# Two on-chip buffers merged, a third ring lengthened, and one small exponential moved in a two-layer graph-attention kernel

## The chip, the cores and the metric

The kernel runs on one core of a Trainium2 chip. Such a core has a matrix engine (PE), which multiplies and whose weight loads are recorded as a row of their own (PEld), a vector engine (DVE), a scalar engine (ACT), a general engine (POOL), and a queue that issues transfers (SP). Each engine works through its own list of instructions in order; engines wait for each other through semaphores. The metric is the device time of one execution in microseconds (us): lower is better. The kernel before takes 2965.63 us (median of three runs, 2965.52 to 2966.96).

## The reference

Sixty-four independent graphs of 256 nodes with 512 features each pass through two layers, and each layer is a residual with a layer norm around it:

```
x = layernorm(x + relu(attention_0(x, adj)))
x = layernorm(x + attention_1(x, nodemask, adj))

attention_0: feats = x W  (8 heads of 64);  s_i = feats.a_self,  n_j = feats.a_neigh
             att = softmax_j(leaky_relu(s_i + n_j, 0.2) where adj, else -1e10);  out = att feats + b
attention_1: q, k, v = x W_qkv  (8 heads of 64)
             att = 0.33 softmax(q k^T / 8) + 0.33 adj + 0.33 exp(-adj);  out = (att v) W_out + b_out
```

All of it is float32.

## The kernel before

One graph is one batch `b`; a batch is 128 partitions by two row tiles. The loop over `b` is a software pipeline: in round `b`, the two functions `attention0_beside_projections1(b)` and `attention1_beside_projections0(b)` run parts of up to five batches beside each other, among them layer 0's attention of batch `b`, layer 1's softmax of batch `b-1`, layer 1's output of batch `b-2` and layer 0's features of batch `b+1`. They are lists of `do(stage, batch, step)` calls, and after every call `in_order()` ties each new instruction behind the one before it on its engine. So the order in which a step stands in the list is the order on PE, ACT, DVE and SP alike. All loads and stores of the loop are issued by SP.

The projections use a scheme with seven products in place of eight (`seven`, lines 292 to 325). Of its products, p1, p6, p7 and p4 are summed up in one PSUM bank, the "chain": after p1 the bank is copied out by ACT (line 320), and only then may PE add p6 into the same bank, and so on. The p2 product has a bank of its own, p5 and p3 share a third. For the output projection (`po`, layer 1's last product) the copies go to the tile `o`; the left factors that are sums, `oC`, are made on DVE in two steps, `half_blocks` 0 and 1 (lines 285 to 290). PE's order in that projection is p1, p2, p6, p5, p7, then the row sums `pd` of the softmax, then p4 and p3.

In the stretch before it, PE computes the scores of layer 1, `pz`, for four pairs of heads g = 0 to 3 (`scores`, line 857), and between g = 1 and g = 2 the products of the previous batch's probabilities with its values (`values`, `av`, line 973). ACT turns each `pz` into `p` with two exponentials (line 871), one for each half of the keys. DVE adds the two halves to `both` (line 883).

The tiles named `p` come from a ring of four buffers with the tag "p". A batch has four of them, one per pair of heads, so the first exponential of a batch waits until `values` has read the first `p` of the batch before.

Layer 0's attention needs factors along the rows of the next batch: PE transposes them (`pr`, line 82), DVE takes a maximum and a bias `nb` from it (lines 499 and 500), ACT forms an exponential of 8 x 256 numbers into `grow` (`broadcast` part 0, line 506), DVE clamps it (`broadcast` part 1, line 510), SP writes it to DRAM (`gs`, line 514) and reads it back spread over all 128 partitions (`gb`, line 515, 1028 KB). The next readers are `nd` (line 559), from which ACT forms `ccol` (line 566), and the weights `pT` (line 667).

The rows of `x` for the residual are loaded by `load_rows` (line 138, 512 KB) into a buffer with the tag "x", of which there is one; they are read by `end` (line 733) in the next round. The tile `hb`, layer 0's output in blocks, has a buffer of its own with the tag "hb"; it is written by four transfers in `blocks` (line 114, from the DRAM copy `hs`) and read by DVE's transpose `hT` (line 121). In the list, `load_rows(b + 1)` stands directly behind `blocks`.

Of the kernel before, what the change touches and what calls it, by code (L numbers as in the profile page):

```python
# [8 lines left out]
FT = mybir.dt.float32  # L9
# [8 lines left out]
def kernel(  # L18
# [30 lines left out]
    P = 128  # L49
    NB, N, F = x.shape  # L50
    H, _, U = w0.shape
    T = N // P
    C = F // P
    HG = H // 2
    UA = U + 1
    UX = U + 2
# [8 lines left out]
    io = ctx.enter_context(tc.tile_pool(name="io", bufs=3))  # L65
    work = ctx.enter_context(tc.tile_pool(name="work", bufs=2))
# [40 lines left out]
    X, XB, ADJB, MROW = {}, {}, {}, {}  # L107
# [26 lines left out]
        nc.sync.dma_start(MROW[b], nodemask[b].partition_broadcast(P))  # L134

    def load_rows(b):
        X[b] = io.tile([P, T, F], FT, tag="x", name=f"x_{b}", bufs=1)
        nc.sync.dma_start(X[b], x[b].rearrange("(t p) f -> p t f", p=P))


    mask_sb = io.tile([NB, N], U8, tag="mask", name="mask_sb", bufs=4)
    nc.sync.dma_start(mask_sb, nodemask)
    X[0] = io.tile([P, T, F], FT, tag="x", name="x_0", bufs=1)
    for t in range(T):
        nc.sync.dma_start(X[0][:, t, :], x[0, t * P : (t + 1) * P, :])
    C2, F2 = C // 2, F // 2

    wf_sb = consts.tile([P, 7, C2, HG, UX], FT, name="wf_sb")
    wf12 = work.tile([P, C2, HG, UX], FT, tag="p", name="wf12", bufs=4)
    wf = [[wf_sb[:, 0], wf12], [wf_sb[:, 1], wf_sb[:, 2]]]  # L150
    def load_wf(engine, g):
        for c in range(C):
# [57 lines left out]
    nc.vector.tensor_scalar_mul(m33, pm, L_BOTH)  # L210


    maskz = io.tile([NB, N], FT, tag="hb", name="maskz", bufs=1)
    nc.vector.transpose(maskz, maskf)
    def right_factors(w, w12):

# [23 lines left out]

    def load_weights1():

        wk1 = work.tile([P, C2, F], FT, tag="p", name="wk1", bufs=4)
        wv12 = work.tile([P, C2, F2], FT, tag="both", name="wv12", bufs=4)
        parts = w_qkv.rearrange("(k c p) (h s u) -> s k c p h u", k=2, p=P, s=3, u=U)

        def get(dst, s, k, heads=slice(0, H)):
            for c in range(C2):
                nc.sync.dma_start(
                    dst[:, c].rearrange("p (h u) -> p h u", u=U), parts[s, k, c][:, heads]  # L250
                )

        get(wqk_sb[:, 0], 0, 0)
        get(wqk_sb[:, 1], 0, 1)
        get(wk1, 1, 0)
        get(wqk_sb[:, 6], 1, 1)
        get(wv_sb[:, 0], 2, 0, slice(0, HG))
        get(wv12, 2, 0, slice(HG, H))
        get(wv_sb[:, 1], 2, 1, slice(0, HG))
        get(wv_sb[:, 2], 2, 1, slice(HG, H))  # L260

        def combine(part):
            q1, q2, s1, s2, s3, s4, k2 = (wqk_sb[:, i] for i in range(7))
            if part == 0:
                nc.vector.tensor_add(s1, wk1, k2)
                nc.vector.tensor_sub(s2, s1, q1)
            elif part == 1:
                nc.vector.tensor_sub(s3, q1, wk1)
            elif part == 2:
                nc.vector.tensor_sub(s4, q2, s2)  # L270
            else:
                right_factors(wv_sb, wv12)
            in_order()

        return combine
# [379 lines left out]
    def attend0(b):  # L655
        pT = {}

        def weights(h):


            tag = "pT" if h < HG else "both" if b > 1 or h > HG + 1 else "p"
            if (b, h) == (0, H - 1):
                pT[h] = work.tile([P, T, N], FT, tag="rec1", name=f"pT_{b}_{h}", bufs=1)
            else:
                pT[h] = work.tile([P, T, N], FT, tag=tag, name=f"pT_{b}_{h}", bufs=4)
            for j in range(T):
                nc.vector.scalar_tensor_tensor(  # L667
                    pT[h][:, j, :],
                    GB[b][h],
                    CCOL[b][:, j, h : h + 1],  # L670
                    AT[b][:, j, :],
                    op0=ALU.max,
                    op1=ALU.mult,
                )

        AV = {}

        def product(g, t):


            if t == 0:
                AV[g] = psum.tile([P, T, F], FT, tag="sc", name=f"av0_{b}_{g}", bufs=2)
            av = AV[g][:, t, : HG * UA].rearrange("p (h u) -> p h u", u=UA)
            half = P // 2
            for k in range(HG):
                h = g * HG + k
                for j in range(T):
                    for r in range(2):
                        i = t * P + r * half
                        matmul(  # L690
                            av[r * half : (r + 1) * half, k, :],
                            pT[h][:, j, i : i + half],
                            V0[b][:, j, h, :UA],
                            start=(j == 0),
                            stop=(j == T - 1),
                        )

        REC0 = {}

        def rec0(g):  # L700
            REC0[g] = small.tile([P, T, HG], FT, tag="rec", name=f"rec0_{b}_{g}")
            av = AV[g][:, :, : HG * UA].rearrange("p t (h u) -> p t h u", u=UA)
            nc.vector.reciprocal(REC0[g], av[:, :, :, U])  # L703

        def norm0(g, t):
            if b not in X1:
                X1[b] = io.tile([P, T, F], FT, tag="x1", name=f"x1_{b}", bufs=1)
            av = AV[g][:, t, : HG * UA].rearrange("p (h u) -> p h u", u=UA)
            if b < 1:
                rec = small.tile([P, HG], FT, tag="rec", name=f"rec0_{b}_{g}_{t}")  # L710
                nc.vector.reciprocal(rec, av[:, :, U])
                s = slice(g * HG * U, (g + 1) * HG * U)
                nc.vector.tensor_mul(
                    X1[b][:, t, s].rearrange("p (h u) -> p h u", u=U),
                    av[:, :, :U],
                    rec.unsqueeze(2).to_broadcast([P, HG, U]),
                )
                return
            for k in range(HG):
                h = g * HG + k  # L720
                nc.scalar.activation(  # L721
                    X1[b][:, t, h * U : (h + 1) * U],
                    av[:, k, :U],
                    AF.Copy,
                    scale=REC0[g][:, t, k : k + 1],
                )

        def end(ts=slice(0, T)):
            if ts.start == 0:
                NORM["l0", b] = LayerNorm(X1[b], b, "l0")  # L730
            ln = NORM["l0", b]
            for t in range(ts.start, ts.stop):
                nc.vector.scalar_tensor_tensor(
                    X1[b][:, t, :],
                    X1[b][:, t, :],
                    0.0,
                    X[b][:, t, :],
                    op0=ALU.max,
                    op1=ALU.add,
                    accum_out=ln.sums[:, t : t + 1],  # L740
                )
            ln.mean(ts)
            if ts.stop == T:
                X.pop(b)

        return dict(
            weights=weights,
            product=product,
            rec0=rec0,
            norm0=norm0,  # L750
            end=end,
            squares=lambda *ts: NORM["l0", b].squares(*ts),
            norm=lambda *ts: NORM["l0", b].apply(*ts),
        )
# [83 lines left out]

    def softmax1(b):
        PROBS[b] = [  # L840
            work.tile([P, 2, T, N], FT, tag="p", name=f"p_{b}_{g}", bufs=4)
            for g in range(HG)
        ]
        both = {}
# [102 lines left out]
    def attend1(b):  # L947
        if b < NB - 1:
            oT = work.tile([P, C, N], FT, tag="oT", name=f"oT_{b}", bufs=1)
        else:  # L950
            oT = io.tile([P, C, N], FT, tag="x", name=f"oT_{b}", bufs=1)
        av = {}

        def weights(g):
# [180 lines left out]
    def do(stage, b, step, *args):  # L1135

        if 0 <= b < NB:
            if (stage, b) not in S:
                S[stage, b] = stages[stage](b)
            S[stage, b][step](*args)  # L1140
            in_order()
# [93 lines left out]
    def attention0_beside_projections1(b):  # L1235
# [69 lines left out]
        do("proj0", b + 1, "product", "p7")  # L1305
        do("attend0", b, "norm")
        do("proj1", b, "blocks")
        if b + 1 < NB:
            load_rows(b + 1)
        do("proj0", b + 1, "add", 22)  # L1310
        do("proj0", b + 1, "product", "p2")
        if b + 2 < NB:
# [8 lines left out]
    def attention1_beside_projections0(b):  # L1321
# [12 lines left out]
        do("softmax1", b - 1, "scores", 2)  # L1334
        do("softmax1", b - 1, "scores", 3, 0)
        do("proj0", b + 1, "rows")
        do("proj0", b + 1, "broadcast", 0)
        do("softmax1", b - 1, "scores", 3, 1)
        do("attend1", b - 2, "half_blocks", 1)
        do("proj0", b + 1, "broadcast", 1)  # L1340
        do("softmax1", b - 1, "both", 2)
        do("softmax1", b - 1, "both", 3)
        do("attend1", b - 2, "product", "p1")
        do("attend1", b - 2, "product", "p2")
        do("proj1", b, "hT")
        do("attend1", b - 2, "product_add", 11)
# [7 lines left out]
        do("attend1", b - 2, "product", "p4")  # L1354
        do("proj0", b + 1, "bias")
        do("softmax1", b - 1, "inverted")
        do("attend1", b - 2, "product", "p3")
        do("attend1", b - 2, "product_add", 12)
        if b == 1:
# [129 lines left out]
```

## Time and profile before

| what | value |
|---|---|
| median of three runs | 2965.63 us |
| the profiled execution, its own time | 2965.2 us |
| its span, first to last instruction | 2963.4 us |
| mean granted PE clock | 0.994 of full speed |
| round of the loop (start of `pz` to start of `pz`, 1491.10 to 1536.09) | 44.99 us |
| mean DMA rate | 122 GB/s |
| the first 150 us: PE clock, PE busy | 0.91, 128.22 us |
| the last 94 us: PE clock, PE busy | 0.94, 80.97 us |

The span is the time from the first to the last instruction of the program; the execution's own time lies 1.8 us above it. The profile shows for each engine how long it was busy, for each wait who ended it, and in the timeline when each group of instructions began. Nearly all of the span is made of 62 like rounds; a time that recurs in every round counts some 62-fold. Times in the prediction such as 1546.21 are microseconds from the start of the span, and most belong to the round that begins at 1536.09.

### The profile page before, as it was taken

What the parts mean: (1) busy time and instruction counts of PE and PEld (TensorE: products, weight loads), DVE (VectorE), ACT (ScalarE), POOL (GpSimd) and SP (SyncE); (2) the same over time, 40 slices, a digit from 0 to 9 for tenths busy, and PEclk for the clock granted to TensorE, in tenths of its full rate; (3) what the DMA queues carried; (4) which work ended last, traced back from release to release, by engine and by line L of the source; (5) the groups of instructions that cost most, each with busy time, mean ns of one, the idle gap of its engine ahead of it and who ended that gap; (6) DMA issues with size and microseconds to landing.
All of it is one profiled execution on the core that took longest, in us unless ns stands there. A gap on an engine that the chain in (4) does not pass through costs nothing.

```text
span 2963.4 us, 67973 instructions
## 1 busy us (share of the span) xinstructions
PE 2906.6 (98%) x26302; PEld 2468.6 (83%) x26302; DVE 2600.9 (88%) x5147; ACT 1779.5 (60%) x4905; POOL 209.9 (7%) x526
## 2 busy tenths in 40 slices
PE   8899999999999999999999999999999999999998
PEld 6788888888888888888888888888888888888886
DVE  5798988988989989989989889889899899899884
ACT  2556665666666666566666656666666666666563
POOL 0000000000000000000000000000000000000001
PEclk8999999999999999999999999999999999999999
DMA  6445445454454454454454554554544544545532
GB/s 126 94 123 123 121 135 123 118 139 114 121 138 116 120 142 115 122 130 119 131 123 119 138 123 115 141 113 121 139 115 120 138 117 125 126 121 133 123 101 68
DMA packets 778872, 362.24 MB, mean 122 GB/s; under 512 B 694604, under 2 KB 696636, under 8 KB 762552
## 3 DMA queue, kind: packets, MB, share of 16 engines
q1 hardware_dynamic: 776440, 357.37, 47.6%
q8 instruction: 210, 3.44, 0.5%
q14 instruction: 110, 0.90, 0.1%
q10 hardware_dynamic: 2112, 0.52, 0.1%
HBM read 289.42 MB, written 68.13 MB: 121 GB/s over the span
## 4 chain that ended last, share of the span: by engine, by line
PE 73%; DMA 12%; ACT 7%; SPq 4%; DVE 3%; issue 1%; POOL 0%; DVEq 0%; ACTq 0%; POOLq 0%
PE pq_p L311 27%; PE pv_p L311 13%; PE po_p L311 10%; PE pf_p L311 9%; PE av L690 8%; DMA x<-in_x_dram 6%; DMA hs<-x 4%; SPq L114 4%; ACT p L871 3%; ACT x L382 2%; PE pd L891 2%; PE pz L857 1%; PE av L973 1%; DVE xT L121 1%; ACT v L320 1%
## 5 line engine op out<-in xcount | busy, mean ns | idle before, releaser
L311 PE MATMUL pq_p<-hC,wqk_sb 128*128 128x128 f32 x4096 | 493.3, 279 | 5.3 <-ACT qk L320 3.6
L311 PEld LDWEIGHTS pq_p<-hC,wqk_sb 128*128 128x128 f32 x4096 | 468.7, 192 | 22.3 <-ACT qk L320 17.7
L667 DVE SCALAR_TENSOR_TENSOR pT<-gb,ccol,at 128x256 f32<-128x256 f32 x992 | 403.0, 477 | 55.3 <-ACT ccol L566 55.3
L871 ACT ACTIVATE p<-pz,hide 128x512 f32<-128x512 f32 x512 | 315.4, 685 | 140.8 <-PE av L973 123.8
L311 PE MATMUL pq_p<-hT,wqk_sb 128*128 128x128 f32 x3072 | 366.2, 276 | 1.4 <-DVE hT L121 0.7
L311 PEld LDWEIGHTS pq_p<-hT,wqk_sb 128*128 128x128 f32 x3072 | 360.1, 193 | 5.5 <-DVE hT L121 1.2
L963 DVE TENSOR_TENSOR p<-p,ct 128x1024 f32<-128x1024 f32 x252 | 308.7, 1225 | 8.6
L721 ACT ACTIVATE x<-av,rec 128x64 f32<-128x64 f32 x1008 | 221.0, 336 | 151.4 <-DVE rec L703 151.4
L956 DVE TENSOR_TENSOR p<-p,rb 128x1024 f32<-128x1024 f32 x252 | 304.2, 1207 | 4.9 <-DMA rb<-rs 4.9
L311 PE MATMUL po_p<-wo_sb,oC 128*128 128x256 f32 x992 | 240.9, 386 | 21.2 <-ACT o L320 21.2
L690 PE MATMUL av<-v,pT 128*64 128x65 f32 x8192 | 256.7, 223 | 1.1 <-DVE pT L667 0.6
L857 PE MATMUL pz<-qk 64*128 64x256 f32 x2048 | 256.2, 389 | 0.9 <-ACT p L871 0.9
L690 PEld LDWEIGHTS av<-v,pT 128*64 128x64 f32 x8192 | 246.9, 138 | 10.2 <-issue 2.5
L626 ACT ACTIVATE v<-v 128x64 f32<-128x64 f32 x1024 | 251.7, 338 | 0.0
L311 PE MATMUL pf_p<-wf_sb,xC 128*128 128x264 f32 x992 | 251.3, 386 | 0.0
L311 PE MATMUL pv_p<-wv_sb,hC 128*128 128x256 f32 x1024 | 244.2, 381 | 4.1 <-ACT v L320 4.1
L857 PEld LDWEIGHTS pz<-qk 64*128 64x128 f32 x2048 | 187.1, 186 | 65.5 <-ACT p L871 26.1
L311 PEld LDWEIGHTS po_p<-wo_sb,oC 128*128 128x128 f32 x992 | 183.3, 190 | 68.7 <-ACT o L320 46.1
L973 PE MATMUL av<-p,v 128*64 128x256 f32 x2016 | 231.9, 382 | 0.2 <-DVE p L963 0.2
L320 ACT COPY v<-pv_p 128x256 f32<-128x256 f32 x256 | 95.6, 373 | 226.1 <-PE pv_p L311 225.9
L883 DVE SCALAR_TENSOR_TENSOR both<-p 128x512 f32<-128x512 f32 x256 | 170.3, 683 | 60.7 <-ACT p L871 60.7
L311 PEld LDWEIGHTS pv_p<-wv_sb,hC 128*128 128x128 f32 x1024 | 195.4, 191 | 32.7 <-ACT v L320 4.9
(163 smaller groups left out, 4453.8 us busy)
## 6 DMA issues: line engine op xcount, KB each, us to landing
rb<-rs SPq DMA_DIRECT2D x63, 1024.0 KB
gb<-gs SPq DMA_DIRECT2D x62, 1028.0 KB
hs<-x SPq DMA_DIRECT2D x64, 512.0 KB
xb<-in_x_dram SPq DMA_DIRECT2D x252, 128.0 KB
x<-in_x_dram SPq DMA_DIRECT2D x63, 512.0 KB
hb<-hs SPq DMA_DIRECT2D x252, 128.0 KB
y<-hs SPq DMA_DIRECT2D x63, 512.0 KB
out_dram<-y SPq DMA_DIRECT2D x63, 512.0 KB
```

The source lines that it names most:

```text
L311: matmul(d, lhsT, rhs, start=(p in FIRST and i == 0), stop=(i == len(todo) - 1), skip_group_check=True,)
L320: nc.scalar.copy(out[COPIES[p]], dst)
L626: nc.scalar.activation(V0[b][:, t, h, :U], V0[b][:, t, h, :U], AF.Copy, scale=V0[b][:, t, h, U : U + 1],)
L667: nc.vector.scalar_tensor_tensor(pT[h][:, j, :], GB[b][h], CCOL[b][:, j, h : h + 1], AT[b][:, j, :], op0=ALU.max, op1=ALU.mult,)
L690: matmul(av[r * half : (r + 1) * half, k, :], pT[h][:, j, i : i + half], V0[b][:, j, h, :UA], start=(j == 0), stop=(j == T - 1),)
L721: nc.scalar.activation(X1[b][:, t, h * U : (h + 1) * U], av[:, k, :U], AF.Copy, scale=REC0[g][:, t, k : k + 1],)
L857: matmul(pz[:, r, j, :], QK[b][rows, g, 1, j * P : (j + 1) * P], QK[b][rows, g, 0, :], start=True, stop=True,)
L871: nc.scalar.activation(p[:, :, j, :], pz[:, :, j, :], AF.Exp, bias=hide[:, j, b : b + 1], scale=U**-0.5,)
L883: nc.vector.scalar_tensor_tensor(both[g], p[:, :, 0, :], TINY, p[:, :, 1, :], op0=ALU.add, op1=ALU.add)
L956: nc.vector.tensor_mul(p, p, REC[b][:, k : k + 2, g // 2, :] .unsqueeze(2) .to_broadcast([P, 2, T, N]),)
L963: nc.vector.tensor_add(p, p, CT[b].unsqueeze(1).to_broadcast([P, 2, T, N]))
L973: matmul(av[0][r * U : (r + 1) * U, g % 2, :], V1[b][:, j, 2 * g + r, :], PROBS[b][g][:, r, j, :], start=(j == 0), stop=(j == T - 1),)
```

## The change

The change has four edits that go together.

1. The ring "p" of layer 1's probabilities gets a fifth buffer.
2. To make room, the tag "x" goes: `x`'s rows now take the same single buffer as `hb` (tag "hb"). The two tiles that had used these buffers at the edges of the program move: `maskz` from "hb" to "y", and the last batch's `oT` from "x" to "xC".
3. Since `x`'s rows of batch b+1 can be written only when `hb` of batch b has been read, `load_rows(b + 1)` moves from behind `blocks` to the end of the round, behind `inverted`, that is behind the transfers `rs` and `rb`.
4. `broadcast` part 0 (the exponential into `grow`) moves from in front of the last exponential of `p` to behind the output projection's p1 with its copy; part 1 (the clamp, and the transfers `gs` and `gb`) moves behind `both` of g = 2. In the list p1 itself moves up, in front of `broadcast`; PE's order stays.

```diff
     def load_rows(b):
-        X[b] = io.tile([P, T, F], FT, tag="x", name=f"x_{b}", bufs=1)
+        X[b] = io.tile([P, T, F], FT, tag="hb", name=f"x_{b}", bufs=1)
         nc.sync.dma_start(X[b], x[b].rearrange("(t p) f -> p t f", p=P))
...
-    maskz = io.tile([NB, N], FT, tag="hb", name="maskz", bufs=1)
+    maskz = io.tile([NB, N], FT, tag="y", name="maskz", bufs=1)
...
         PROBS[b] = [
-            work.tile([P, 2, T, N], FT, tag="p", name=f"p_{b}_{g}", bufs=4)
+            work.tile([P, 2, T, N], FT, tag="p", name=f"p_{b}_{g}", bufs=5)
             for g in range(HG)
         ]
...
-            oT = io.tile([P, C, N], FT, tag="x", name=f"oT_{b}", bufs=1)
+            oT = work.tile([P, C, N], FT, tag="xC", name=f"oT_{b}", bufs=1)
...
         do("proj1", b, "blocks")
-        if b + 1 < NB:
-            load_rows(b + 1)
         do("proj0", b + 1, "add", 22)
...
         do("softmax1", b - 1, "scores", 3, 0)
         do("proj0", b + 1, "rows")
-        do("proj0", b + 1, "broadcast", 0)
         do("softmax1", b - 1, "scores", 3, 1)
         do("attend1", b - 2, "half_blocks", 1)
+        do("softmax1", b - 1, "both", 2)
+        do("attend1", b - 2, "product", "p1")
+        do("proj0", b + 1, "broadcast", 0)
         do("proj0", b + 1, "broadcast", 1)
-        do("softmax1", b - 1, "both", 2)
         do("softmax1", b - 1, "both", 3)
-        do("attend1", b - 2, "product", "p1")
         do("attend1", b - 2, "product", "p2")
...
         do("softmax1", b - 1, "inverted")
+        if b + 1 < NB:
+            load_rows(b + 1)
         do("attend1", b - 2, "product", "p3")
```

The lines left out change the first batch's `x_0` to the tag "hb" and `bufs=4` to `bufs=5` at the other tiles of the ring "p". No arithmetic is added or taken away. On ACT the order of a round was: both exponentials of g = 2, the first of g = 3, `grow`, the second of g = 3, copy of product p1. It becomes: both of g = 2, both of g = 3, copy of product p1, `grow`. On DVE it was: `half_blocks` 1, clamp, `both` 2, `both` 3. It becomes: `half_blocks` 1, `both` 2, clamp, `both` 3.

More of the change, by code (lines that the diff above doesn't have):

```diff
@@ L142 @@
     nc.sync.dma_start(mask_sb, nodemask)
-    X[0] = io.tile([P, T, F], FT, tag="x", name="x_0", bufs=1)
+    X[0] = io.tile([P, T, F], FT, tag="hb", name="x_0", bufs=1)
     for t in range(T):
@@ L148 @@
     wf_sb = consts.tile([P, 7, C2, HG, UX], FT, name="wf_sb")
-    wf12 = work.tile([P, C2, HG, UX], FT, tag="p", name="wf12", bufs=4)
+    wf12 = work.tile([P, C2, HG, UX], FT, tag="p", name="wf12", bufs=5)
     wf = [[wf_sb[:, 0], wf12], [wf_sb[:, 1], wf_sb[:, 2]]]
@@ L241, in load_weights1 @@
     def load_weights1():
-        wk1 = work.tile([P, C2, F], FT, tag="p", name="wk1", bufs=4)
+        wk1 = work.tile([P, C2, F], FT, tag="p", name="wk1", bufs=5)
         wv12 = work.tile([P, C2, F2], FT, tag="both", name="wv12", bufs=4)
@@ L664, in weights @@
             else:
-                pT[h] = work.tile([P, T, N], FT, tag=tag, name=f"pT_{b}_{h}", bufs=4)
+                pT[h] = work.tile(
+                    [P, T, N], FT, tag=tag, name=f"pT_{b}_{h}", bufs=5 if tag == "p" else 4
+                )
             for j in range(T):
```

## The prediction

> **What bounds the kernel now.** First the page's part 1 (busy time by engine), then the waits (total us, times, longest).
>
> ```profile
> PE 2906.6 (98%) x26302; PEld 2468.6 (83%) x26302; DVE 2600.9 (88%) x5147; ACT 1779.5 (60%) x4905; POOL 209.9 (7%) x526
> ```
>
> ```profile
> ACT p L871 <- PE av L973: 123.8, 61, 2.0
> ...
> PE po_p L311 <- ACT o L320: 21.2, 62, 0.7
> ...
> PE pv_p L311 <- ACT v L320: 5.0, 4, 2.3
> ...
> DVE nd L559 <- DMA gb<-gs: 3.6, 7, 1.0
> ```
>
> PE sets the time. Only one of its waits recurs in every round: 62 times before `po_p`, for ACT's copy `o`. The idle column gives 0.34 us each, but the ends of matmuls are modelled, so I measure from start to start, in PE's timeline (start, length, group):
>
> ```profile
> 1523.72 1.89 PE L311 MATMUL pv_p<-wv_sb,hT 128*128 128x256 f32 x8
> 1525.45 2.75 PE L311 MATMUL pv_p<-wv_sb,hC 128*128 128x256 f32 x12
> 1528.04 1.05 PE L311 MATMUL pf_p<-wf_sb,xT 128*128 128x264 f32 x4
> ...
> 1543.99 1.89 PE L311 MATMUL po_p<-wo_sb,oT 128*128 128x256 f32 x8
> 1546.21 2.86 PE L311 MATMUL po_p<-wo_sb,oC 128*128 128x256 f32 x12 [0.33 <-ACT o L320]
> 1549.00 1.07 PE L891 MATMUL pd<-both,ones 128*32 128x256 f32 x16
> ```
>
> Two projections of the same form. `pv_p` runs unhindered: eight records in 1525.45 - 1523.72 = 1.73 us, 0.216 each, twelve in 2.59. `po_p` takes 2.22 for its eight (0.49 more) and 2.79 for its twelve (0.20 more). Of that 0.20 I put half to the restart behind the stop and half to the change of shape at `pd`: where `po_p` restarts behind `pd` without waiting for ACT, its four records take 1505.98 - 1505.01 = 0.97 instead of 0.86, so a restart costs 0.10. **The stop thus costs 0.49 + 0.10 = 0.59 us a round, 62 x 0.59 = 36.6 us**, not the 21.2 of the idle column.
>
> Why ACT is late (ACT's timeline of that stretch):
>
> ```profile
> 1542.80 1.84 ACT L871 ACTIVATE p<-pz,hide 128x512 f32<-128x512 f32 x3 [0.27 <-PE pz L857]
> 1544.87 0.47 ACT L506 ACTIVATE grow<-pr,nb 8x256 f32<-8x256 f32 x1 [0.22 <-issue]
> 1545.24 0.66 ACT L871 ACTIVATE p<-pz,hide 128x512 f32<-128x512 f32 x1
> 1545.81 0.34 ACT L320 COPY o<-po_p 128x256 f32<-128x256 f32 x1
> 1547.38 0.37 ACT L320 COPY o<-po_p 128x256 f32<-128x256 f32 x1 [1.22 <-PE po_p L311]
> ```
>
> `grow` waits 0.22 for its bias `nb` (DVE, 1544.64 + 0.14) and then takes a slot; the last exponential and the copy stand behind it.
>
> **The moved exponential.** Back-to-back exponentials start 0.57 apart (four in 2.42, the next ACT group 2.29 behind the first: 1539.15 to 1541.44). The three from 1542.80 last to 1544.64, so the third (0.69 long) starts at about 1543.96. Without `grow` the fourth starts at 1544.53, not 1545.24, and the copy at 1545.10, not 1545.81. The copy's input is there: p1 is the first four of PE's eight records, over at 1543.99 + 3 x 0.216 + 0.38 = 1545.02. It ends at 1545.44, and with today's hand-off (1546.15 to 1546.21) PE may go on at 1545.50. Unhindered, p6's matmul is due at 1543.99 + 8 x 0.216 = 1545.72, and its weight load one slot ahead, at 1545.50. **So the stop goes whole, with no margin left for the weight load**; a slip of 0.1 would cost up to 6 us of the 36.6. What is late next on PE: p7's wait for p6's copy. It passes unhindered today (twelve records without an inner gap beyond those named), and keeps its distance, since p6's end and its copy move together; `grow` (about 1545.4 to 1545.9) is over before the copy of p6 at about 1546.8.
>
> **What stands behind `grow`.** DVE: clamp (0.27), `both` 3, the transpose `hT`. DVE now takes `both` 2 (0.67) at 1545.38 and reaches the clamp at about 1546.0, when `grow` is done; the same three operations fill the same time, and `hT` starts at 1546.79 as before. Cost 0. DVE also has 1.19 us idle at 1549.5 before the next `o` sum (it waits for ACT's copy of p7); 0.59 of it goes, so it does not bound.
>
> SP: `gs` starts at 1546.3 instead of 1545.68, 0.62 later, and `nd` is wanted 0.59 earlier:
>
> ```profile
> 1541.02 0.67 SPq L138 DMA_DIRECT2D x<-in_x_dram  x1
> 1541.79 2.62 SPq L114 DMA_DIRECT2D adj<-in_adj_dram  x4
> 1544.45 0.74 SPq L134 DMA_DIRECT2D mask<-in_nodemask_dram  x1
> 1545.68 0.31 SPq L514 DMA_DIRECT2D gs<-grow  x1
> 1547.59 0.34 SPq L515 DMA_DIRECT2D gb<-gs  x1
> ...
> 1554.55 0.16 DVE L559 TENSOR_TENSOR nd<-v,gb 128x16 f32<-128x16 f32 x1
> ```
>
> From `gs` to `gb` 1.91; from `gb`'s issue to `nd`, in rounds where `nd` did wait for it, 5.5 to 5.9 (1419.99 - 1414.44 in one), 7.3 and 7.5 in two of them. So `nd` can start at 1546.3 + 1.9 + 5.7 = 1553.9, and is wanted at 1553.96. Beyond that it has cover: `ccol` starts only at 1555.44, behind ACT's `qk` copy, 0.73 behind `nd`'s end, so about 0.65 of lateness costs nothing; then `pT`, whose last ends at 1562.7 for the matmul that reads it at about 1563.8, about 1 us more. Cost 0, though `nd`'s 7 waits will be more.
>
> **x's rows.** Their issue (0.67) and 512 KB leave the stretch in front of `gs`: its DMA share is 0.92 (1541.0 to 1547.6). In some rounds SP itself brings `gs` late (1591.61, 1.2 behind its clamp), and there the missing issue gives back what the clamp takes. The new place is behind `rb`, at about 1556 in this round's terms, where DMA stands at 0.54 and then 0.01 (1566.0 to 1575.3). `rb`, wanted at 1565.27, is issued before x (1556.08) and is waited for once in the whole span. The store `out` and the load `y` behind x come 1.5 to 2 us later (that stretch moves 182 GB/s at a share of 0.54, some 340 KB per us at full share, and x has 512 KB); `y` is issued at 1562.39 and wanted at 1572.17: covered.
>
> Here a rule speaks against the change. The Trainium skill, "Trainium Kernel Development and Optimization", section Best Practices, wants buffers doubled so that DMA and compute overlap; the shared buffer does the reverse: x can't land before `hT` has read `hb`, nor `hb` before `end` has read x. By the rule a load of 4.2 us (x's step in the chain of waits, 1541.02 to 1545.24) would be exposed: 62 x 4.2 = 260 us slower. By the row, x's first reader starts at 1570.61, 14 us behind the new issue, and `hb`'s transfers at 1538.22 come 12 us after that reader in their round. I take 0. (That step itself is an inferred link: in the next round x is issued at 1587.23 and the copy still comes 3.6 us later, so nothing on ACT waits for x.)
>
> **The fifth buffer.** It ends ACT's 2.03 us wait in front of the first exponential (61 in 123.8 us). "Perfetto Trace Analysis", section Optimization Strategy, reads a gap that recurs on the engine that should be saturated as a sign of too little SBUF; taken for ACT that would promise 124 us. But ACT is 60% busy, and by the rows nothing on PE comes sooner: scores of g = 2 start at 1541.62, directly behind `values`, and the exponential at 1542.80 waits for those scores. Value 0; DVE gets its first two `both` up to 1 us earlier, and waits for PE's `pr` instead.
>
> **Sum**: 2965.2 (the profiled execution) - 36.6 = 2928.6; the median lies 0.4 above it, and I leave 1 us for slips at the weight load: **2930 us**.
>
> **Rivals.**
>
> *The gain is given back at the next hand-off* (10%). PE already waits a little for ACT's `qk` copy before `pq`'s p6 (1555.59; 17.7 us in all on the weight load). If ACT's chain there (`zd`, copy, two squares, `qk`) kept its times, PE would lose again what it gained: 2965, or 2947 if half. Against it: `zd` waits for DVE's `inv`, which follows the `o` sum, which follows PE's p7; that chain moves with PE.
>
> *A smaller slip at the copy* (within the 80% below): if ACT's copy, now the first to carry the wait for the transpose of `xb`, comes 0.1 to 0.2 late, 62 x 0.1 to 0.2 comes back: 2935 to 2941.
>
> *Slower through `gb`* (4%). Place: `nd`. Its price is 62 us for each us beyond cover. It decides once `gs`-to-`gb`-to-`nd` takes over 1553.96 + 0.65 + 1.0 - 1546.3 = 9.3 us in most rounds (8.6 to 9.8 with the roughness of the cover), and makes the kernel slower than before once it also eats 0.59, at 9.9; at 10.5 the time is 2965 + 37 = 3002. For: two rounds had 7.5 behind `gb` alone. Against: the usual 7.4 to 7.8, and a less loaded stretch.
>
> *The change does nothing* (4%): `grow` only trades places and the copy is held by something the trace puts down to ACT: 2965.
>
> **Numbers.** Whole or nearly whole gain 80%, given back in part 6%, in whole 4%, nothing 4%, slower by `gb` or a transfer 4%, more than the stop (rounds at the DMA-late end gain too, up to 2922) 2%. The range runs from 2924 to 2946. A measurement tells 0.2% (6 us) from no change: faster 0.88, same 0.08, slower 0.04.
>
> **What would show it.** Right: PE's wait for `o` gone from its list; `po_p`'s eight records 1.73 apart from the twelve; round 44.4; ACT's first exponential 2 us earlier without effect; `nd` waiting for `gb` in many rounds, by under 0.7. Wrong: the stop unchanged or moved to `pq_p`; `pT` or `av` (line 690) waiting for `gb`; `end` (line 733) waiting for x.

## The result, and the profile after

The changed kernel takes 2945.48 us (median of four runs, 2943.05 to 2947.07); the kernel before, measured again beside it, 2966.15. The ratio is 0.9929, with a 95% interval of 0.9912 to 0.9947. So it is faster by 20.7 us, inside the stated range but 0.5 us below its upper end, where 36.6 us had been forecast as the gain of the path. The profiled execution of the changed kernel has a span of 2943.7 us (2945.5 us in all), at a granted clock of 0.994 as before.

The page after, parts 1 and 4:

```profile
PE 2893.2 (98%) x26302; PEld 2475.2 (84%) x26302; DVE 2595.7 (88%) x5147; ACT 1784.6 (61%) x4905; POOL 210.1 (7%) x526
...
PE 95%; DVE 2%; issue 1%; DMA 1%; ACT 1%; SPq 0%; POOL 0%; DVEq 0%; POOLq 0%; ACTq 0%
```

The chain that ended last now stays on PE for 95% of the span, where it was 73%: the link over ACT's copy, and with it the links over transfers that had been inferred behind it, are gone. The same place in PE's timeline of the changed kernel, in the same round of the loop:

```profile
1532.16 1.89 PE L311 MATMUL po_p<-wo_sb,oT 128*128 128x256 f32 x8
1533.89 2.75 PE L311 MATMUL po_p<-wo_sb,oC 128*128 128x256 f32 x12
1536.58 1.07 PE L893 MATMUL pd<-both,ones 128*32 128x256 f32 x16
```

The eight records and the twelve are 1.73 us apart, as `pv_p`'s are, and no idle time stands behind the line. ACT in that stretch:

```profile
1530.97 2.42 ACT L873 ACTIVATE p<-pz,hide 128x512 f32<-128x512 f32 x4 [0.48 <-PE pz L859]
1533.27 0.39 ACT L320 COPY o<-po_p 128x256 f32<-128x256 f32 x1
1533.52 0.46 ACT L506 ACTIVATE grow<-pr,nb 8x256 f32<-8x256 f32 x1
```

Four exponentials in one piece, then the copy, then `grow`. The usual round, from `pr` to `pr`, is 44.39 us long; it was 44.98. The difference of 0.59, in 62 rounds, is the 36.6 us of the forecast. But the span shrank by 19.7 only. What took the rest is in the waits (total us, times, longest):

```profile
ACT p L873 <- PE av L975: 37.3, 61, 0.6
...
PE av L692 <- issue: 12.6, 9, 2.1
...
DVE nd L559 <- DMA gb<-gs: 3.9, 9, 0.8
...
PE pq_p L311 <- issue: 2.0, 2, 1.2
```

Two lines are new: PE stops 11 times on "issue", 14.6 us of idle in all, some 16.8 from start to start. "Issue" is time in which an engine waits for no instruction that the profile shows. One of the stops, in PE's timeline:

```profile
1548.73 3.95 PE L692 MATMUL av<-v,pT 128*64 128x65 f32 x128
1552.61 0.38 PE L311 MATMUL pq_p<-hC,wqk_sb 128*128 128x128 f32 x1
1554.20 1.94 PE L311 MATMUL pq_p<-hC,wqk_sb 128*128 128x128 f32 x15 [1.21 <-issue]
```

The sixteen matmuls of one product are broken after the first; those behind it need nothing that the first did not have. It is no wait for data. All of these stops lie 21 to 23 us behind the round's `pr`, and they come 4, 7 or 11 rounds apart. What lies there among the transfers (SP's timeline, then three stretches: window, length, busy time of PE, PEld, DVE, ACT and POOL, PE clock, DMA share, GB/s):

```profile
1543.66 0.31 SPq L939 DMA_DIRECT2D rb<-rs  x1
1544.02 0.43 SPq L138 DMA_DIRECT2D x<-in_x_dram  x1
1545.78 0.39 SPq L1113 DMA_DIRECT2D out_dram<-y  x1
1552.42 0.36 SPq L989 DMA_DIRECT2D y<-hs  x1
```

```profile
1544.40:1548.50 4.10, 4.10 (x39) 4.10 (x38) 4.10 (x11) 4.10 (x13) 0.00 (x0) 1.00 0.93 265
1548.50:1552.20 3.70, 3.70 (x121) 3.58 (x121) 3.39 (x9) 2.03 (x8) 0.00 (x0) 1.00 0.86 277
1552.20:1555.60 3.40, 2.19 (x31) 1.93 (x26) 3.37 (x7) 1.75 (x8) 0.00 (x0) 1.00 0.45 157
```

`rb`, x's rows and the store follow each other without a pause for over 7 us, and PE runs dry at the end of that burst. The page's part 3 lists the queue q8, kind "instruction", with 210 packets and 3.44 MB, 16384 bytes a packet. PE's records show that these are PE's own instructions, 256 to a packet. From one stop to the next PE goes through 3328, 5888 or 9216 records (matmuls, weight loads and its waits for semaphores), which is exactly 13, 23 or 36 times 256, and just as many packets of q8 start in between. So every stop lies at a seam between two packets' worth of instructions; in the other kernels below that stop, all stops lie on the same seams. A round has 836 records, 3.27 packets' worth, so a seam comes back to nearly the same place of the round after 4, 7 or 11 rounds. Counting q8's packets, in 60 rounds, by the time since the round's `pr`:

```
started in            before   changed
12.0 to 19.0 us         30        14
19.0 to 21.0 us         23        58
21.0 to 23.0 us         42         3
```

In the changed kernel the burst ends about 20 us behind `pr`, hardly a packet of instructions starts while it lasts (8 in 61 bursts, their last microsecond left out), and 58 start within the 2 us around its end. Each of the stops ends 2.2 to 2.5 us after such a packet has begun (1551.87 for the one shown).

The length of a burst alone does not bring a stop. The longest burst of a round in the kernel before was another one, with `hb`, x and `adj`, in front of `gs`. It lasted 8.1 us (median), over 7.2 us in 58 of 59 rounds, and stopped nothing. A stretch of it (same columns as above):

```profile
1541.00:1547.60 6.60, 6.27 (x42) 4.59 (x39) 6.00 (x13) 4.89 (x10) 0.00 (x0) 1.00 0.92 171
```

Counting records from the seams tells when PE needs a packet. Packets that start during that burst, or within 1 us of its end, still come 12.8 us or more before that; at the burst behind `rb` in the changed kernel the least is 2.2 us. The two places differ in how fast PE uses its instructions: in the row just shown it goes through 42 matmuls and 39 weight loads in 6.60 us, in the first two rows of the stretch behind `rb` through 160 and 159 in 7.80 us, and `av` alone takes a packet's worth (128 matmuls and their 128 weight loads) in 3.95 us. So a late packet is missed where PE uses its instructions fastest.

### The profile page after: what moved, and what is told of

It is laid out like the page before. It is cut to its first block, busy times and chain, and to the rows that moved or that the text cites. A ratio compares the mean times of both kernels' runs of the same rounds, so it can differ in the third digit from the quotient of the medians.

```text
span 2943.7 us, 67840 instructions
## 1 busy us (share of the span) xinstructions
PE 2893.2 (98%) x26302; PEld 2475.2 (84%) x26302; DVE 2595.7 (88%) x5147; ACT 1784.6 (61%) x4905; POOL 210.1 (7%) x526
## 3 DMA queue, kind: packets, MB, share of 16 engines
q8 instruction: 210, 3.44, 0.5%
## 4 chain that ended last, share of the span: by engine, by line
PE 95%; DVE 2%; issue 1%; DMA 1%; ACT 1%; SPq 0%; POOL 0%; DVEq 0%; POOLq 0%; ACTq 0%
PE pq_p L311 27%; PE pf_p L311 13%; PE pv_p L311 13%; PE po_p L311 13%; PE av L692 9%; PE pz L859 8%; PE av L975 7%; PE pd L893 2%; PE pr L82 1%; PE po L1096 0%; PE pg L548 0%; SPq L114 0%; DMA gb<-gs 0%; DMA x<-in_x_dram 0%; ACT junk L363 0%
## 5 line engine op out<-in xcount | busy, mean ns | idle before, releaser
L311 PE MATMUL po_p<-wo_sb,oC 128*128 128x256 f32 x992 | 234.5, 379 | 0.5 <-ACT o L320 0.5
L311 PEld LDWEIGHTS pf_p<-wf_sb,xC 128*128 128x128 f32 x992 | 187.8, 190 | 31.5 <-ACT v L320 0.3
```

What stands on the lines that cost most here:

```text
L311: matmul(d, lhsT, rhs, start=(p in FIRST and i == 0), stop=(i == len(todo) - 1), skip_group_check=True,)
```

## The experiments

**Theory 1**: the fourth edit (the exponential) is worth the whole 36.6 us, and the third (x's rows behind `rb`) costs about 15, since the longer burst of transfers holds up PE's instructions. **Theory 2**: the shorter round itself brings the stops. **Theory 3**: the fifth buffer carries part of the gain. Each kernel was timed beside the kernel before on the same chip; "ratio" is to that. The first four runs shared one measurement of it (2964.97 us), the last four another (2962.90).

**The exponential alone.** The kernel before with the fourth edit as the diff above shows it, and none of the others.

> The kernel before with the fourth edit alone (the exponential into grow behind p1's copy); x's rows keep their own buffer and their place behind the blocks, four buffers for p. Theory 1 (the part of the gain that is missing is lost because x's 512 KB now stand behind rb and hold up PE's instruction fetch): the whole stop at po_p's p6 goes and no other comes, 2966 - 36.6 = 2929 to 2931 us, no wait of PE on 'issue' at av or pq_p. Theory 2 (the shorter round itself brings the new stops, wherever x is loaded): 2945, with some 10 waits of PE on 'issue'. Theory 3 (the fifth buffer carries part of the gain): slower than the changed kernel, above 2947.

Measured: 2928.92 us, ratio 0.9881 (0.9867 to 0.9894). Its waits:

```profile
DVE nd L559 <- DMA gb<-gs: 18.4, 24, 1.4
...
PE av L690 <- issue: 1.2, 3, 0.5
```

The whole gain, with next to no stop on "issue", and with four buffers and the old place for x. Theory 2 falls, since the round here is just as short (44.39). So does theory 3. The first line is the cover of the forecast put to use: with x still in front of `gs`, `nd` waits for `gb` in 24 rounds, up to 1.4 us, and the time does not show it.

**Everything but the exponential.** The changed kernel with the fourth edit undone:

```diff
         do("proj0", b + 1, "rows")
+        do("proj0", b + 1, "broadcast", 0)
         do("softmax1", b - 1, "scores", 3, 1)
         do("attend1", b - 2, "half_blocks", 1)
+        do("proj0", b + 1, "broadcast", 1)
         do("softmax1", b - 1, "both", 2)
-        do("attend1", b - 2, "product", "p1")
-        do("proj0", b + 1, "broadcast", 0)
-        do("proj0", b + 1, "broadcast", 1)
         do("softmax1", b - 1, "both", 3)
+        do("attend1", b - 2, "product", "p1")
```

> The changed kernel with the fourth edit undone: fifth buffer, merged buffer and x's rows behind rb, but grow's exponential where it was. Theory 1: the stop at p6 stays and the new stops come on top, 11 of about 1.4 us: 2966 + 15 = 2981 us (2974 to 2986). Theory 2: 2966, no new waits of PE on 'issue'. Theory 3: below 2964.

Measured: 2981.14 us, ratio 1.0058 (1.0045 to 1.0071): slower than before. Its waits have both stops, the old and the new:

```profile
PE po_p L311 <- ACT o L320: 20.0, 62, 0.5
...
PE av L692 <- issue: 12.6, 10, 2.0
```

With the run above this splits the change into two parts that add up: -36 and +16 on 2964.97 make 2945, the changed kernel's time.

**x's rows at another place.** Only the place of `load_rows` is changed; the merged buffer stays.

```diff
             do("attend1", b - 3, "rows_again")
+            load_rows(b)
             do("proj1", b - 1, "qk", "p6")
...
         do("softmax1", b - 1, "inverted")
-        if b + 1 < NB:
-            load_rows(b + 1)
```

> The changed kernel with x's rows issued behind the load of y (one place further on, in the next round), where the DMA engines have been idle. Theory 1: rb and the store are no longer followed by x without a break, the stops on 'issue' go: 2929 to 2932 us. Theory 2: 2945 as the changed kernel. If x comes too late there, the sum over x (DVE, x<-x,x) waits for DMA x in the list of waits and the time is above 2932.

Measured: 2925.91 us, ratio 0.9867 (0.9852 to 0.9882). That is 3 us below the range expected. All but two of the stops are gone:

```profile
PE av L692 <- issue: 0.7, 2, 0.5
```

x's first reader waits for it once, 0.4 us, although it is issued some 6.5 us later. This version beats the kernel before and the changed one; it cannot be told apart from the exponential alone.

**Four buffers for p**, once in the changed kernel and once in the last one: `bufs=5` becomes `bufs=4` at all tiles of the ring.

> The changed kernel with four buffers for p again, all else as changed. Theory 1 and 2: the fifth buffer is worth nothing on PE, 2945 as the changed kernel (2942 to 2948), ACT waits about 2 us a round for av in front of the first exponential again. Theory 3: slower than the changed kernel by more than 4 us.

> x's rows behind the load of y as in the run x_behind_y, but with four buffers for p. If the fifth buffer is worth nothing on PE: the same as x_behind_y, 2923 to 2929 us. If it carries something once the stops on 'issue' are out of the way: 2930 or more.

Measured: 2947.58 us (2938.57 to 2951.24) beside the changed kernel's 2945.48, and 2927.29, ratio 0.9878 (0.9865 to 0.9892), beside 2925.91. Neither pair can be told apart. With four buffers ACT again waits 123.9 us in all for `av`, and PE's usual round is 44.39 us all the same: the fifth buffer takes 87 us of waiting off an engine that does not bound.

**Other data at the same place.** The last kernel (x behind `y`, four buffers), with a load added behind `rb` that is no part of the computation:

```diff
         do("softmax1", b - 1, "inverted")
+        if b + 1 < NB:
+            extra = io.tile([P, T, F], FT, tag="x", name=f"extra_{b}", bufs=1)
+            nc.sync.dma_start(extra, x[b + 1].rearrange("(t p) f -> p t f", p=P))
+            in_order()
```

> The run x_behind_y_four with one more load of 512 KB behind rb, at the place where the changed kernel loads x: the same rows of x into a tile of its own that nobody reads, in the space that the fifth buffer had. Theory 1 (an unbroken burst behind rb holds up PE's instruction fetch, whoever needs its data): about 11 stops of 1.4 us on 'issue' return, 2926 + 15 = 2941 us (2937 to 2946). Rival (the stops come from x's own waits: its shared buffer, or readers that wait for it): as x_behind_y_four, 2923 to 2929.

Measured: 2946.59 us, ratio 0.9941 (0.9929 to 0.9954), 0.6 us above the range expected.

```profile
PE av L692 <- issue: 12.6, 8, 1.9
DVE x L735 <- DMA x<-in_x_dram: 7.3, 11, 2.1
...
PE pq_p L311 <- issue: 1.9, 3, 0.9
```

DVE's sum over x, whose load now stands behind one more transfer, waits in 11 rounds. The time does not show it: the profiled execution is 15.6 us longer than that of the same kernel without the added load, and PE's stops account for 15.8 (table below). Data that nobody waits for bring the stops back at their full size. So neither the merged buffer nor x's readers are the cause.

**Half of x at that place.**

```diff
     def load_rows(b):
         X[b] = io.tile([P, T, F], FT, tag="hb", name=f"x_{b}", bufs=1)
-        nc.sync.dma_start(X[b], x[b].rearrange("(t p) f -> p t f", p=P))
+        load_half(b, 0)
+        if b == 1:
+            load_half(b, 1)
+
+    def load_half(b, t):
+        nc.sync.dma_start(X[b][:, t, :], x[b, t * P : (t + 1) * P, :])
...
             do("attend1", b - 3, "rows_again")
+            load_half(b, 1)
```

> The changed kernel with x's rows in two halves of 256 KB: the first stays behind rb, the second goes behind the load of y. Theory 1: the burst is about 0.75 us shorter, each of the 11 stops too, and the shortest vanish: 4 to 9 us of stops left, 2930 to 2936 us. Rival (a further transfer at that place costs the same whatever its size): 2941 to 2947.

Measured: 2933.76 us, ratio 0.9898 (0.9883 to 0.9914). The amount counts. Put together, with the length of the burst that begins at `rb` (from its first packet to the first pause of 0.25 us, median over the rounds), the gaps of PE above 0.45 us that lie 19.5 to 24 us behind `pr`, and their sum beyond the usual pace, all counted from the packets and records of one profiled execution each:

```
kernel                    burst us   stops   sum us   time us
before                      4.98       0       0      2962.9 to 2966.2
exponential alone           5.05       3       1.8    2928.92
x behind y                  5.06       2       1.1    2925.91
x behind y, four buffers    5.17       1       0.9    2927.29
half of x                   6.27       7       5.4    2933.76
changed                     7.23      11      16.8    2945.48
other data                  7.35      11      16.7    2946.59
changed, four buffers       7.30      14      18.9    2947.58
no exponential              7.28      13      17.4    2981.14
```

At this place of the round the sum grows with the burst, and more than in proportion: from 5.0 to 6.3 us of burst it gains some 4 us, from 6.3 to 7.2 another 11.

**A miss: ACT's squares behind the copy.** PE has a last stop that recurs, 0.19 us at `pq`'s p6 and 0.10 of restart, because ACT's two squares of layer 1's output (line 363) stand in front of the copy `qk`. In the version with x behind `y` they were moved:

```diff
-            do("attend1", b - 4, "squares")
             do("proj1", b - 1, "qk", "p1")
+            do("attend1", b - 4, "squares")
             do("proj1", b - 1, "qk", "p2")
```

> The run x_behind_y with ACT's two squares of layer 1's output (line 363, y) moved from in front of the copy of pq's p1 to behind it. PE's last recurring stop, 0.19 + 0.10 us at pq's p6 in every round, should go: 60 x 0.3 = 18 us, 2908 us (2904 to 2914). If the squares then make ccol or the store late, or another wait takes its place: 2920 or more.

Measured: 2950.04 us, ratio 0.9950 (0.9938 to 0.9963): some 24 us slower than the version it started from (ratio 0.9867). ACT and PE in one round:

```profile
1543.71 0.59 ACT L320 COPY qk<-pq_p 128x512 f32<-128x512 f32 x1 [0.30 <-PE pq_p L311]
...
1547.36 1.52 ACT L382 ACTIVATE y<-y,shift_l,rstd_l 128x512 f32<-128x512 f32 x2 [1.27 <-POOL shift_l L378]
1548.79 0.56 ACT L320 COPY qk<-pq_p 128x512 f32<-128x512 f32 x1
```

```profile
1545.30 3.74 PE L311 MATMUL pq_p<-hC,wqk_sb 128*128 128x128 f32 x32
1549.40 0.82 PE L311 MATMUL pq_p<-hC,wqk_sb 128*128 128x128 f32 x5 [0.36 <-ACT qk L320]
```

The first copy of `qk` is early now and p6 goes through (1545.30, directly behind p2). But the squares lead, over POOL, to the scaling of `y` (line 382), which stands in front of the next copy of `qk` on ACT; so PE stops at p7 instead, from start to start 0.53 us longer and with 0.10 of restart. The round is 44.73 us, 0.34 more, which in 62 rounds is 21 of the 24 us.

## Why the prediction was right or wrong

Right: the stop at `po_p`'s p6, why it was there, and its price from start to start. 0.59 us a round was forecast, and 44.98 - 44.39 measured; the exponential alone gave 2928.92 against a sum of 2928.6. The idle column's 21.2 us would have been 15 too low. The weight load kept its slot with no loss: the 1 us put aside for slips was not needed.

Right: nothing on DVE or at `nd` was late enough to show in the time. Wrong in detail: `nd` was to wait for `gb` in many rounds, but it did in only 9, because with x gone from that stretch `gs` passed to `gb` in 1.33 us (median) instead of the 1.91 that the sum took from a row with x in front. In the run that kept x there, 24 rounds waited, and the cover held.

Right: the fifth buffer is worth nothing on PE, though it takes away most of ACT's longest wait of that stretch (37.3 us are left of 123.8). Right too that the rival at the next hand-off would not come: `pq`'s p6 waits as much as before (its start-to-start excess is 0.19 in both), since ACT's chain moved with PE.

**Wrong: the step on x's rows, "I take 0."** The term was mis-sized by the 15 to 16 us that the median lies above the forecast of 2930. The step asked who waits for x, for `rb`, for `out` and for `y`, and all of these were covered, as the runs confirm. It did not ask who else uses the same transfers. It also read the room behind `rb` from a mean, a DMA share of 0.54 over 11.7 us; by the packets it was one burst of 4.99 us (1557.04 to 1562.03) at a share of 0.87, and about 0.3 in the rest. x lengthened such bursts to over 7 us, and the only reader without cover was PE's own instruction stream, which at `av` needs a new packet within 4 us. No rival named it: the one that put the loss on a transfer put it on `gb`. That the time still fell inside the range is luck: its upper part stood for a slip at the copy or a gain given back at the next hand-off, and neither came.

The double-buffering rule of the Trainium skill ("Trainium Kernel Development and Optimization", Best Practices) spoke against the change and by its reason promised 260 us of loss. The loss came from the same edit, but not for that reason: with the merged buffer kept and x one place further on, the median is the lowest of all, 2925.91.

Left open: by what path the instruction packets come to wait for the end of a burst. The trace shows when they start and on which queue, but not what they queued behind. That the place of the burst matters beside its length rests on two bursts of each round and on the counted records; no run moved a long burst on purpose to a place where PE uses its instructions slowly.

## What to carry to other kernels

Price a stall of PE from start to start against an unhindered group of the same form, since the idle column leaves out the restart and part of the stop. A transfer that nobody waits for is not free of charge: before moving one, look for the stretch in which the matrix engine goes through most instructions in a microsecond (here many small matmuls, `av`), and do not lengthen a run of transfers that ends there. The longest run of transfers need not be the one that costs: here it lay elsewhere and cost nothing. And where a change couples a gain with a cost, run the parts alone: here the small part carried all of the gain, and the part that looked like housekeeping took over two fifths of it back.

## What the runs showed of the hardware

PE can run dry of instructions in a kernel whose transfers take only 48% of the engines' time. Bursts of 7.2 us that ended about where PE goes through 256 instructions in 3.95 us stopped it in 11 of 62 rounds, by 1.5 us on average (16.8 us in all). Bursts of 5 us at that place left next to nothing, and bursts of 8.1 us where PE went through some 80 instructions in 6.6 us stopped nothing. PE's instructions came in packets of 16384 bytes, 256 to a packet. The profile calls such a stop "issue" and names no releaser for it, and it may fall in the middle of one product. The signs are its place at the end of a burst and a distance between stops of a whole number of times 256 of PE's records.
